# Order of the output products, the 64-row convolution block and the gates in half of the kernel's unit pairs

## The chip, the cores and the metric

The kernel runs on one core of a Trainium2 chip. The metric is device microseconds of one execution, the median of several runs. Lower is better.

## The reference

The input is x, 4 images of 128 channels of 96 x 96. Each image is normalised in 32 groups, then read as four sequences of 9216 positions: by rows, by rows backward, by columns, by columns backward. Every sequence goes through the same block, and the four results are fused by a 1x1 convolution and added to x. The block, cut to what matters:

```python
t = _grouped1x1(x, in_proj_w, in_proj_b, G)
u, gate = (t[:, :HID], t[:, HID:])
u = silu(u)
u = conv1d(u, dw_w, groups=HID)              # 5 taps, per channel
s = _conv1x1(u, ssm_in_w)
a = clip(DMIN + (DMAX - DMIN) * sigmoid(_conv1x1(u, ssm_delta_w, ssm_delta_b)))
bb, cc = tanh(_conv1x1(u, ssm_b_w, ssm_b_b)), tanh(_conv1x1(u, ssm_c_w, ssm_c_b))
hst = exp(prefix) * cumsum(bb * s * exp(-prefix))    # prefix = cumsum(log(a))
u = u + _conv1x1(cc * hst + ssm_d * s, ssm_out_w)
u = _grouped1x1(u * sigmoid(gate), mix_w, mix_b, G)
return _conv1x1(u, out_proj_w, out_proj_b)
```

## The kernel before, in words

**Tiling.** A sequence is cut into 6 stages per phase, and a stage's positions into 4 residues modulo 4 (`R`). One unit is one residue of one stage of one direction: 384 positions by 256 channels, held as two halves `j` of 128 channels. Units come in pairs, one forward and one backward (`s` = 0 and 1). Eight phases (4 images, two reading orders) of 6 stages of 4 pairs make 192 pairs; `pair` runs the first six, `pair_on` the others, one after another. The order of everything is written out by hand under a manual schedule: each engine runs its instructions in the order in which the code issues them.

**What a pair does in `pair_on`.** In the order of the code: the front of a pair four places on (`front`, where it is still to be computed); the five taps of the convolution of half 1 on VectorE and ScalarE (`taps`, L744 and L742); the convolution of half 0 on TensorE, eight products of 128 rows (`conv`, the tile `band`); the recurrence; the copies `under` (L589), which put u of an older pair `bi` into the banks 0 to 3, so that the output of the recurrence is added there; two output products (`add_next`, which calls `accumulate`: eight matmuls with `w_fin` each, and a ScalarE copy `ys` at L862 or L860, which GpSimd or VectorE later adds to `acc`, L879); the rest of the convolution (`conv_less`, the tile `less`, 64 rows) and its copy into u (`copy_u`, L717); the gates' products (`gate`, L557) and the recurrence's output products (`out_of`, L577), each of 32 rows and 128 columns; the gating on VectorE (`gating`, L638); the gates' tanh on ScalarE (L593, L599); and the projection of the new u (`proj`, the tile `main`, 16 products).

**Which pairs.** `fronted` is true where the front is still to be computed, in the first three stages of a phase as seen four pairs ahead. In the other pairs the silu tiles are reused or reloaded, and these compute gates for a pair further on (`gated`). `single` is true for the residues 0 and 3: there half 0 needs just one block of the convolution, and VectorE adds the edge (L691). For the residues 1 and 2 the 64-row block `conv_less` is needed, accumulating into the same banks.

**Banks.** PSUM has 8 banks. In pairs that are not fronted the convolution is in banks 6 and 7, the output products in 4 and 5 (`PROJ`), which the projection uses later; the recurrence's output goes to 0 to 3. The gates go to banks 4 (1, 1), 7 (1, 0), 6 (0, 0) and 5 (0, 1). `copy_u` takes banks 6 and 7 in one copy of 128 x 768.

**Shapes on TensorE.** A matmul takes as many rows of the array as its contraction has, and as many columns as its output has. `accumulate`, `conv` and `proj` are 128 rows by 32 columns, four beside each other; `conv_less` is 64 by 32, eight beside each other; `gate` and `out_of` are 32 by 128, four beside each other, one in each row group. `gate(s, j)` is in row group 2(1 - s) + j, `out_of(s, j)` in row group 2j + s.

Of the kernel before, what the change touches and what calls it, by code (L numbers as in the profile page):

```python
# [68 lines left out]
def conv_preact_kernel(  # L69
# [55 lines left out]
    def bank(i):  # L125
        return psum[:, i, :]

    def mm(o, col, lhsT, rhs, start, stop):
        r = slice(32 * col, 32 * col + 32)
        nc.tensor.matmul(o[r, : rhs.shape[-1]], lhsT, rhs, start=start, stop=stop,  # L130
                         skip_group_check=True)
# [166 lines left out]
    def fresh(step):  # L298

        return step * UB < NU and step % NS < NS // 2  # L300
# [72 lines left out]
    def less_of(p):  # L373
        return 1 if p < 2 else 0

    def less_rows(s, p):
        low = 64 * ((less_of(p) + s + 1) % 2)
        return slice(low, low + 64)
# [174 lines left out]
    def gate(bi, s, j, to):  # L553
        un = units[bi]
        q, off = gate_at(un)
        r = slice(64 * (1 - s) + 32 * j, 64 * (1 - s) + 32 * j + 32)
        nc.tensor.matmul(bank(to)[:, :N], stats[un["b"]][0][r, s, :], x_in[s][r, q, off : off + N],  # L557
                         start=True, stop=True)
# [10 lines left out]
    def ssm(bi, s):  # L569

        k = bi - NU + 8 + s
        return turning[k % 3] if bi >= NU - 8 else SSM + 2 * s

    def out_of(bi, s, j):
        z = tbs[bi]
        r = slice(64 * j + 32 * s, 64 * j + 32 * s + 32)
        nc.tensor.matmul(bank(ssm(bi, s) + j)[:, :N], w_so[r, bass.ts(j, P)], z[r, :],  # L577
                         start=(bi, s) not in seeded, stop=True, skip_group_check=True)
# [7 lines left out]
    def under(bi, s):  # L586

        seeded.add((bi, s))
        nc.scalar.copy(psum[:, ssm(bi, s) : ssm(bi, s) + 2, :N], us[bi][:, s])  # L589
# [52 lines left out]
    def columns(step, sil, k):  # L642

        if fresh(step):
            return sil[..., k : k + N]
        return sil[..., 1 - k : 1 - k + N][..., ::-1]

    def blocks(step):
        return [sils[step][:, s if fresh(step) else 1 - s, 0] for s in range(2)]
# [10 lines left out]
    def alone(p):  # L660
        return p in (0, R - 1)
# [38 lines left out]
    def conv_less(i, banks, copy=True):  # L700
        step, p = units[i]["step"], units[i]["p"]
        sil, k, b0 = blocks(step), less_of(p), min(banks)
        for g in range(4):
            for s in range(2):
                r = less_rows(s, p)
                mm(bank(b0 + s), g, less[r, p, g, :], columns(step, sil[s][r, g, :], k),
                   False, True)
        if copy:
            copy_u(i, banks)

    def copy_u(i, banks):
        b0 = min(banks)
        if banks == PROJ:
            for s in range(2):
                nc.scalar.copy(us[i][:, s, 0, :], bank(b0 + s)[:, :N])
        else:
            nc.scalar.copy(us[i][:, :, 0, :], psum[:, b0 : b0 + 2, :N])  # L717
# [82 lines left out]
    def scale_s(i):  # L800
        s = tbs[i][0:64, :]
        nc.scalar.activation(s, s, AF.Copy, scale=d_sb[0:64, 0:1])
# [92 lines left out]
    def piece(t, place):  # L895
        later.pop((t % NP, place), lambda: None)()
# [58 lines left out]
    def pair_on(t):  # L955
        i, k, n, end = 2 * t, t % R, t - LAG, NU // 2
        bi, last = 2 * n, t == end - 1
        late = n > 1 and (n - 1) % (NP * 2) == 0
        un = units[i]
        single = alone(un["p"])  # L960
        step, g = divmod(t + R, R)
        fronted, gated = fresh(step), None
# [9 lines left out]
        banks, w = (PROJ, FRONT[:2]) if fronted else ((6, 7), PROJ)  # L972
# [31 lines left out]
        def add_next(bk):  # L1004
            if n:
                add = accumulate(waiting.pop(0), bk, *adder)
                held.append(add) if late or k == R - 1 and not last else add()

        add_next(w[0])
        if not fronted:  # L1010
            if not single:
                conv_less(i, banks, False)
            under(bi, 0)
            if not single:
                copy_u(i, banks)
        add_next(w[1])
        if fronted:
            if not single:
                conv_less(i, banks)
            if t % NP == 20:  # L1020
                scale_s(i - 4)
            scale_s(i - 2)

        def gate_of(s, j, bk):
            if gated is not None:
                gate(2 * gated, s, j, bk)
# [2 lines left out]
        out_of(bi, 0, 0)  # L1029
        out_of(bi, 0, 1)  # L1030
        out_of(bi, 1, 1)
        gate_of(1, 0, 7)
        gate_of(0, 0, 6)
        out_of(bi, 1, 0)
        gate_of(0, 1, 5)
        piece(t, 1)
        for s in range(2):
            gating(bi, s)
# [245 lines left out]
    with tc.manual_schedule(  # L1284
        engines={
            nc.tensor.engine, nc.vector.engine, nc.scalar.engine, nc.gpsimd.engine, nc.sync.engine
        }
    ):
        start()
        for t in range(LAG):  # L1290
            pair(t)
        for t in range(LAG, NU // 2):
            pair_on(t)
        tail()
# [82 lines left out]
```

## Time and profile before

| | |
|---|---|
| median of 3 runs | 1737.27 us (1737.03 to 1740.41) |
| span of the profiled execution | 1735.2 us |
| TensorE matmuls busy (PE) | 1713.6 us, 99% |
| weight loads (PEld) | 644.7 us, 37% |
| VectorE (DVE) | 1507.9 us, 87% |
| ScalarE (ACT) | 1494.8 us, 86% |
| GpSimd (POOL) | 1447.0 us, 83% |
| granted TensorE clock | 1.000 |

The profile gives the span, from the first to the last instruction, and no other time of that execution. A row of the timeline has the start in us, the length in us, the engine, the line of the kernel, the operation, the tiles (out<-in), shapes and the count of instructions that are merged in it; in brackets stands how long the engine was idle before it and what ended that. A row that merges matmuls goes from the first start to the last modelled end.

### The profile page before, as it was taken

How to read it: one execution, taken by the hardware profiler on the slowest of the kernel's cores; microseconds unless marked ns; L12 is line 12 of the kernel's file. 1: busy time of each engine (PE TensorE's matmuls, PEld its weight loads, DVE VectorE, ACT ScalarE, POOL GpSimd, SP SyncE). 2: the span in 40 equal slices, each digit the busy share in tenths (PEclk: the TensorE clock that was granted, in tenths of full speed). 3: DMA queues.
4: the chain of work that ended last, by engine and by line, in shares of the span. 5: the costliest groups of instructions: out<-in, count | busy, mean ns of one | idle time of the engine just before them, and what ended most of it. 6: DMA issues, size and time to landing. Idle time of an engine off the chain costs nothing.

```text
span 1735.2 us, 54226 instructions
## 1 busy us (share of the span) xinstructions
PE 1713.6 (99%) x22522; PEld 644.7 (37%) x22522; DVE 1507.9 (87%) x1508; ACT 1494.8 (86%) x2544; POOL 1447.0 (83%) x1490
## 2 busy tenths in 40 slices
PE   7999999999999999999999999999999999999998
PEld 4333333343333433344333443334333333333333
DVE  6899998888889998888889999888888888888887
ACT  4888988889888888888988888888998889888875
POOL 3689889888789988888788988887878889887887
PEclk9999999999999999999999999999999999999999
DMA  7746865358884786337896487433887548643364
GB/s 244 235 147 218 288 202 151 124 206 280 275 287 139 262 267 194 118 126 263 260 308 226 150 300 251 144 123 132 294 294 239 179 144 304 201 137 133 147 226 166
DMA packets 154644, 363.66 MB, mean 210 GB/s; under 512 B 19104, under 2 KB 120864, under 8 KB 154400
## 3 DMA queue, kind: packets, MB, share of 16 engines
q1 hardware_dynamic: 154256, 360.16, 62.8%
q8 instruction: 178, 2.92, 0.7%
q14 instruction: 66, 0.54, 0.1%
q10 hardware_dynamic: 144, 0.04, 0.0%
HBM read 221.41 MB, written 138.53 MB: 207 GB/s over the span
## 4 chain that ended last, share of the span: by engine, by line
PE 95%; DVE 2%; ACT 1%; DMA 1%; issue 0%; SPq 0%; DVEq 0%; ACTq 0%
PE psum L130 81%; PE psum L577 8%; PE psum L557 5%; DVE psum L744 1%; PE psum L1188 0%; DMA acc<-in_xr 0%; DMA kept<-shared 0%; DVE u L638 0%; ACT psum L589 0%; ACT psum L742 0%; DVE u L744 0%; ACT sil L527 0%; SPq L335 0%; PE psum L1195 0%; DVE u L691 0%
## 5 line engine op out<-in xcount | busy, mean ns | idle before, releaser
L744 DVE SCALAR_TENSOR_TENSOR psum<-sil,small,psum 128x768 f32<-128x768 f32 x576 | 589.1, 1023 | 42.2 <-ACT psum L742 16.8
L130 PE MATMUL psum<-u,w_fin 128*32 128x384 f32 (+1 forms) x6192 | 541.3, 484 | 1.1 <-ACT ys L860 0.4
L130 PE MATMUL psum<-u,main 128*32 128x384 f32 x6144 | 535.0, 489 | 0.5 <-DVE u L691 0.4
L638 DVE SCALAR_TENSOR_TENSOR u<-gate,psum 128x768 f32<-128x768 f32 x376 | 341.7, 950 | 150.0 <-PE psum L577 50.8
L879 POOL TENSOR_TENSOR acc<-ys,acc 128x384 f32<-128x384 f32 x375 | 411.8, 1120 | 14.0 <-ACT ys L860 1.9
L825 POOL TENSOR_TENSOR t<-t,t 64x384 f32<-64x384 f32 (+1 forms) x192 | 287.2, 1496 | 70.6 <-DVE t L819 48.3
L589 ACT COPY psum<-u 128x768 f32<-128x768 f32 x384 | 301.4, 799 | 10.5 <-DVE u L638 4.3
L130 PEld LDWEIGHTS psum<-u,w_fin 128*32 128x32 f32 x6192 | 195.2, 109 | 309.6 <-issue 235.5
L130 PEld LDWEIGHTS psum<-u,main 128*32 128x32 f32 x6144 | 180.0, 109 | 324.5 <-issue 218.3
L130 PE MATMUL psum<-sil,band 128*32 128x384 f32 x3072 | 285.3, 488 | 0.0
L792 POOL TENSOR_SCALAR t<-tm 64x384 f32<-64x384 f32 x184 | 170.8, 928 | 114.4 <-ACT tm L781 102.4
L826 POOL TENSOR_TENSOR t<-t,t 64x384 f32<-64x384 f32 (+1 forms) x192 | 233.9, 1218 | 15.1
L793 POOL TENSOR_TENSOR t<-t,tm 64x384 f32<-64x384 f32 x192 | 213.8, 1113 | 30.2 <-ACT t L784 15.5
L577 PE MATMUL psum<-t,main 32*128 32x384 f32 x1536 | 228.1, 525 | 4.2 <-ACT psum L589 4.2
L742 ACT ACTIVATE psum<-sil,small 128x768 f32<-128x768 f32 x191 | 172.6, 904 | 65.2 <-DVE u L638 61.9
L744 DVE SCALAR_TENSOR_TENSOR u<-sil,small,psum 128x768 f32<-128x768 f32 x192 | 194.9, 1015 | 6.8
L527 ACT ACTIVATE sil<-psum,bnorm 128x385 f32<-128x385 f32 x384 | 191.6, 584 | 4.0 <-DMA edge<-sil 0.9
L557 PE MATMUL psum<-x_in,wn 32*128 32x384 f32 x768 | 161.7, 498 | 0.0
L862 ACT COPY ys<-psum 128x384 f32<-128x384 f32 x288 | 132.3, 478 | 33.0 <-PE psum L130 28.3
L130 PEld LDWEIGHTS psum<-sil,band 128*32 128x32 f32 x3072 | 88.8, 108 | 171.4 <-issue 63.1
L781 ACT ACTIVATE tm<-psum,small 128x384 f32<-128x384 f32 x192 | 110.9, 578 | 14.0 <-PE psum L130 2.3
L577 PEld LDWEIGHTS psum<-t,main 32*128 32x128 f32 x1536 | 93.9, 183 | 73.7 <-issue 41.0
(108 smaller groups left out, 1512.3 us busy)
## 6 DMA issues: line engine op xcount, KB each, us to landing
gate<-kept SPq DMA_DIRECT2D x114, 768.0 KB, 5.2
kept<-gate SPq DMA_DIRECT2D x74, 768.0 KB, 3.7
sil<-sil SPq DMA_DIRECT2D x64, 770.0 KB, 6.6
lone<-edge SPq DMA_DIRECT2D x40, 770.0 KB, 7.5
x_in<-in_xs SPq DMA_DIRECT2D x250, 96.2 KB, 3.3
edge<-sil SPq DMA_DIRECT2D x96, 192.5 KB, 3.6
out<-acc SPq DMA_DIRECT2D x46, 384.0 KB, 6.4
acc<-in_xr SPq DMA_DIRECT2D x39, 384.0 KB, 6.4
```

What stands on the lines that cost most here:

```text
L130: nc.tensor.matmul(o[r, : rhs.shape[-1]], lhsT, rhs, start=start, stop=stop, skip_group_check=True)
L527: nc.scalar.activation(sils[step][:, s, j, g, :], bank(bk)[:, : N + 1], AF.Silu, bias=bn[:, 1:2] if j else bn[:, 4 + g : 5 + g],)
L557: nc.tensor.matmul(bank(to)[:, :N], stats[un["b"]][0][r, s, :], x_in[s][r, q, off : off + N], start=True, stop=True)
L577: nc.tensor.matmul(bank(ssm(bi, s) + j)[:, :N], w_so[r, bass.ts(j, P)], z[r, :], start=(bi, s) not in seeded, stop=True, skip_group_check= ...
L589: nc.scalar.copy(psum[:, ssm(bi, s) : ssm(bi, s) + 2, :N], us[bi][:, s])
L638: nc.vector.scalar_tensor_tensor(v, g, 1.0, pz, ALU.add, ALU.mult)
L742: nc.scalar.activation(part, src, AF.Copy, scale=w_tap[:, 0:1])
L744: nc.vector.scalar_tensor_tensor(us[i][:, :, 1, :] if k == K - 1 else part, src, w_tap[:, k : k + 1], part, ALU.mult, ALU.add,)
L793: nc.gpsimd.tensor_mul(ta[0:64, p, :], tb[0:64, :], tm[0:64, :])
L825: engine.tensor_mul(ta[0:64, p, r], tb[64:P, r], ta[64:P, p, r])
L826: engine.tensor_add(tb[0:64, r], ta[0:64, p, r], tb[0:64, r])
L879: adder.tensor_add(part, y, part)
```

## The change

In pairs that are neither fronted nor single, `conv_less` and `copy_u` move behind the second output product, so that both output products stand ahead of the 64-row block and that block directly ahead of the gates. In the same pairs the order of gates and outputs behind it becomes: gate (1, 1); outputs (0, 0), (0, 1), (1, 1), (1, 0); gate (0, 1); and last gates (0, 0) and (1, 0), into the banks 6 and 7 that `copy_u` empties. Single and fronted pairs keep their order.

```diff
         add_next(w[0])
         if not fronted:
-            if not single:
-                conv_less(i, banks, False)
             under(bi, 0)
-            if not single:
-                copy_u(i, banks)
         add_next(w[1])
+        if not fronted and not single:
+            conv_less(i, banks, False)
+            copy_u(i, banks)
...
         out_of(bi, 0, 0)
         out_of(bi, 0, 1)
         out_of(bi, 1, 1)
-        gate_of(1, 0, 7)
-        gate_of(0, 0, 6)
-        out_of(bi, 1, 0)
-        gate_of(0, 1, 5)
+        if single:
+            gate_of(1, 0, 7)
+            gate_of(0, 0, 6)
+            out_of(bi, 1, 0)
+            gate_of(0, 1, 5)
+        else:
+            out_of(bi, 1, 0)
+            gate_of(0, 1, 5)
+            gate_of(0, 0, 6)
+            gate_of(1, 0, 7)
```

On TensorE, one such pair, before; w_fin is the output products, less the 64-row block, x_in the gates (71 for s = 1, 70 for s = 0), t the recurrence's outputs, main the projection, and the brackets name the engines or DMA queues whose semaphore an instruction waits for:

```order
L130 MATMUL psum<-u_1_3_0_904,w_fin 32x384 [waits DVE_49,Activation_49]
L130 MATMUL psum<-u_1_3_0_904,w_fin 32x384 x7
L130 MATMUL psum<-sil_747,less 32x384 x8
L130 MATMUL psum<-u_1_3_0_904,w_fin 32x384 [waits DVE_49,Activation_49]
L130 MATMUL psum<-u_1_3_0_904,w_fin 32x384 x7
L557 MATMUL psum<-x_in_71,wn_269 128x384 [waits DMAHW2_49,Activation_49]
L577 MATMUL psum<-t_0_1_0_0_1036,main 128x384 [waits Activation_49,Pool_49]
L577 MATMUL psum<-t_0_1_0_0_1036,main 128x384 [waits Pool_49]
L577 MATMUL psum<-t_0_1_0_0_1036,main 128x384
L557 MATMUL psum<-x_in_71,wn_269 128x384 [waits Activation_49]
L557 MATMUL psum<-x_in_70,wn_269 128x384 [waits DMAHW1_49]
L577 MATMUL psum<-t_0_1_0_0_1036,main 128x384
```

The last gate, (0, 1), and the projection follow. The same pair in the changed kernel, on TensorE:

```order
L130 MATMUL psum<-u_1_3_0_904,w_fin 32x384 [waits DVE_49,Activation_49]
L130 MATMUL psum<-u_1_3_0_904,w_fin 32x384 x7
L130 MATMUL psum<-u_1_3_0_904,w_fin 32x384 [waits DVE_49,Activation_49]
L130 MATMUL psum<-u_1_3_0_904,w_fin 32x384 x7
L130 MATMUL psum<-sil_747,less 32x384 x8
L557 MATMUL psum<-x_in_71,wn_269 128x384 [waits DMAHW2_49,Activation_49]
L577 MATMUL psum<-t_0_1_0_0_1036,main 128x384 [waits Activation_49,Pool_49]
L577 MATMUL psum<-t_0_1_0_0_1036,main 128x384 [waits Pool_49]
L577 MATMUL psum<-t_0_1_0_0_1036,main 128x384 x2
L557 MATMUL psum<-x_in_70,wn_269 128x384 [waits DMAHW1_49,Activation_49]
L557 MATMUL psum<-x_in_70,wn_269 128x384 [waits Activation_49]
L557 MATMUL psum<-x_in_71,wn_269 128x384
```

The 64-row block has moved behind the second product; the gate that waits for the copy of banks 6 and 7 is now the last but one before the projection, behind all four outputs, and it waits for ScalarE alone.

On ScalarE, at the same place of an earlier pair, L589 is the copy `under`, L862 the copy of an output product, L717 the copy of banks 6 and 7, and L593 a gate's tanh; - is before, + is changed:

```order
 L862 COPY ys_0_2_0_1091<-psum 128x384
 L589 COPY psum<-u_0_3_0_577 128x2x384
+L862 COPY ys_0_2_1_1103<-psum 128x384
 L717 COPY u_2_1_0_1064<-psum 128x2x384
-L862 COPY ys_0_2_1_1112<-psum 128x384
 L593 ACTIVATE gate_177<-psum,bnorm_272 128x384 x2
```

The copy of the second output product now stands ahead of the copy of banks 6 and 7, and that copy directly ahead of the gates' tanh. On VectorE and GpSimd the order of instructions is as before.

## The prediction

> **What bounds the kernel now.** I read the page first, then PE's list of waits, then the timeline of one of the pairs that the change touches, and last the timelines of two kinds of pair that it leaves alone, because they already show the new sequence and the new kind of wait.
>
> ```profile
> span 1735.2 us, 54226 instructions
> PE 1713.6 (99%) x22522; PEld 644.7 (37%) x22522; DVE 1507.9 (87%) x1508; ACT 1494.8 (86%) x2544; POOL 1447.0 (83%) x1490
> ...
> PE 95%; DVE 2%; ACT 1%; DMA 1%; issue 0%; SPq 0%; DVEq 0%; ACTq 0%
> ```
>
> ```profile
> PE psum L577 <- ACT psum L589: 4.2, 6, 1.3
> ```
>
> PE is busy for 99% of the span and carries 95% of the chain that ended last. Apart from one 11.7 us load at the start, its longest total wait is 4.2 us. So a change counts by what it does to PE's own sequence. "Busy" hides two things, though: time lost where the array goes from one tile shape to another, and time in which only some of the four row groups work. Both must be read from start times.
>
> This is a touched pair. PE rows first, then ScalarE (ACT) and VectorE (DVE), all from the timeline:
>
> ```profile
> 301.19 1.47 PE L130 MATMUL psum<-u,w_fin 128*32 128x384 f32 x16
> 302.59 0.88 PE L130 MATMUL psum<-sil,less 64*32 64x384 f32 x16
> 303.39 1.50 PE L130 MATMUL psum<-u,w_fin 128*32 128x384 f32 x16
> 304.82 0.58 PE L557 MATMUL psum<-x_in,wn 32*128 32x384 f32 x1
> 305.25 0.80 PE L577 MATMUL psum<-t,main 32*128 32x384 f32 x4
> 305.58 0.52 PE L557 MATMUL psum<-x_in,wn 32*128 32x384 f32 x3
> 305.90 0.51 PE L557 MATMUL psum<-x_in,wn 32*128 32x384 f32 x3
> 306.40 2.79 PE L130 MATMUL psum<-u,main 128*32 128x384 f32 x32
> ...
> 303.54 0.80 ACT L589 COPY psum<-u 128x768 f32<-128x768 f32 x1
> 304.28 0.79 ACT L717 COPY u<-psum 128x768 f32<-128x768 f32 x1
> 304.97 0.48 ACT L862 COPY ys<-psum 128x384 f32<-128x384 f32 x1
> 305.76 1.31 ACT L593 ACTIVATE gate<-psum,bnorm 128x384 f32<-128x384 f32 x2 [0.31 <-PE psum L577]
> 305.91 1.82 DVE L638 SCALAR_TENSOR_TENSOR u<-gate,psum 128x768 f32<-128x768 f32 x2 [0.56 <-ACT ys L862]
> ```
>
> The trace shows each matmul call as two passes (8 calls, x16), and a block's modelled end lies 0.07 us behind the next block's start (301.19 + 1.47 = 302.66 against 302.59). I count from the first output product, call it 0: the 64-row block starts at 1.40, the second product at 2.20, the gates at 3.63, the projection (u,main) at 5.21. The gate block takes 1.58. Its second half, where a row group gets its second call, starts 0.76 after the first (305.58).
>
> All 47 touched pairs with gates look like this one. The first and the last of them run from first product to projection in 95.04 - 89.81 = 5.23 and 1644.16 - 1638.94 = 5.22; I use 5.22.
>
> ```profile
> 89.81 1.47 PE L130 MATMUL psum<-u,w_fin 128*32 128x384 f32 x16
> 95.04 0.53 PE L130 MATMUL psum<-u,main 128*32 128x384 f32 x4
> ```
>
> ```profile
> 1638.94 1.47 PE L130 MATMUL psum<-u,w_fin 128*32 128x384 f32 x16
> 1644.16 0.53 PE L130 MATMUL psum<-u,main 128*32 128x384 f32 x4
> ```
>
> **The change, part by part.** The instructions are the same in number and kind; nothing is added. `alone` and `fresh` pick the pairs: not fronted and not single are 50 pairs, of which 47 compute gates and 3 at the end of the program don't. This row counts them (51 copies, one of them from the start-up):
>
> ```profile
> L717 ACT COPY u<-psum x51: 792/802/804, 33.1 to 1684.3; 128x768 f32<-128x768 f32 x51
> ```
>
> *What goes: a change of tile shape.* Before, the sequence of shapes is 128x32, 64x32, 128x32, 32x128; now it is 128x32, 64x32, 32x128. The fronted pairs already run it so:
>
> ```profile
> 406.54 2.76 PE L130 MATMUL psum<-u,w_fin 128*32 128x384 f32 x32
> 409.23 0.88 PE L130 MATMUL psum<-sil,less 64*32 64x384 f32 x16
> 410.03 0.93 PE L577 MATMUL psum<-t,main 32*128 32x384 f32 x8
> 410.19 0.86 ACT L715 COPY u<-psum 128x384 f32<-128x384 f32 x2
> ```
>
> There the 64-row block starts 2.69 after the first product and the 32-row block 0.80 after that, at 3.49 instead of 3.63. So the gates would start 0.14 us earlier. If nothing else moved, the projection would start at 3.49 + 1.58 = 5.07, which is 0.15 less than 5.22.
>
> *What comes: a wait for the copy.* The 64-row block ends the convolution in banks 6 and 7. ScalarE copies both out in one instruction (L717), and only then may gates be written there. Before, the second product (1.43 us) stood between the block and the gates, so the copy ended at 305.07, before the first gate into these banks at 305.25 to 305.58. That cover is gone. The new place of the copy is read from the fronted pair: its copy starts at 410.19, 0.09 behind the block's modelled end, that is 3.65 after the first product. ScalarE is free by then: its copy into the accumulating banks (L589) ends at 304.34, 3.15 after the first product, and the second product's copy (L862, 0.48) ends at about 3.6. With 0.80 for L717 the banks are free at 4.45.
>
> Now the release. A gate waiting for a ScalarE copy loaded its weights here, 0.05 after that copy's end (304.97 + 0.48 = 305.45):
>
> ```profile
> 305.50 0.18 PEld L557 LDWEIGHTS psum<-x_in,wn 32*128 32x128 f32 x1
> ```
>
> And this is what follows such a load in an idle row group, in a single pair whose output products waited for a copy that ended at 356.88:
>
> ```profile
> 356.07 0.81 ACT L589 COPY psum<-u 128x768 f32<-128x768 f32 x1
> ```
>
> ```profile
> 356.99 0.47 PEld L577 LDWEIGHTS psum<-t,main 32*128 32x128 f32 x7
> ```
>
> ```profile
> 357.42 0.66 PE L577 MATMUL psum<-t,main 32*128 32x384 f32 x4
> ```
>
> From load to second pass it is 0.43. The second pass takes 0.48 to its modelled end, and the projection starts 0.07 before that, plus 0.01 for the second of the two gates. So the projection starts at 4.45 + 0.05 + 0.43 + 0.48 + 0.01 - 0.07 = **5.35**, against 5.22: **+0.13 us a pair**. Unhindered, the second half would have started at 3.49 + 0.76 = 4.25; its weights now come at 4.50, so the wait of some 0.25 costs more than the crossing gains.
>
> The bounds of this unknown: nothing of the wait felt gives -0.15; and the release at 0.11 behind the copy (356.88 to 356.99, a product that waits for two engines) instead of 0.05 gives +0.19. I take 0.05, since the new first gate behind the copy waits for ScalarE alone, as the one at 305.50 did in that step.
>
> *The rest costs nothing.*
>
> ```profile
> 301.70 0.58 ACT L790 ACTIVATE t<-psum,small 64x384 f32<-64x384 f32 x1
> ```
>
> The second product starts 0.8 us earlier than before, when its bank must be free: the last reader, the tanh L790, ended at 301.70 + 0.58 = 302.28 in this pair, and the product would start at 301.19 + 1.29 = 302.48 (two products take 2.69 with the crossing, one 1.40, so one alone 1.29). The tanh of the first gate (L593, 0.58) now starts behind the copy at 4.45 and ends at about 5.03, ahead of 5.35, so the projection's bank is free. VectorE's gating (L638) needs the first-half products, which come 0.14 earlier. No DMA moves past another on its queue. On ScalarE two copies change places; behind them stand the gates' tanhs, done in time as said.
>
> *The three pairs without gates.* Their projection reads the copied tile at once. Before it is 1652.55 - 1648.05 = 4.50 from the first product; now 4.45 + 0.05 = 4.50. Nothing.
>
> ```profile
> 1648.05 1.47 PE L130 MATMUL psum<-u,w_fin 128*32 128x384 f32 x16
> 1652.55 2.79 PE L130 MATMUL psum<-u,main 128*32 128x384 f32 x32
> ```
>
> **The sum**: 47 x 0.13 = +6.1 us. The span goes from 1735.2 to 1741.3. The profile gives no other time of its own execution; the median of the timed runs, 1737.27, lies 2.1 above the span, and I keep that distance: **1743.4 us**, 0.35% slower. A measurement of this kernel can tell about 0.2% (3.5 us) from no change, so the sign hangs on more than 0.07 us a pair.
>
> **The rivals.**
>
> *Weights in early (no difference).* If the waiting gate's weights were already in the array when the copy ends, the two passes would follow each other as in an unbroken stream, 0.32 apart (305.58 to 305.90) instead of 0.43. That takes 0.11 off: +0.02 a pair, +1 us, 1738.3. Against it: the load itself stood behind the semaphore at 305.50. I give it 0.10. The Trainium skill, "TensorE: Matmul & The Clock Gate", section Architectural detail, says that PE's queue can pull weight loads ahead of matmuls in flight; if that held across a wait for a semaphore, the time would be this rival's 1738.3, while by the row it is the forecast's.
>
> *The copy doesn't hold (faster).* One mechanism: the gates into banks 6 and 7 stand last, six calls behind the block, and if ScalarE were done before their turn, only the crossing would be left. It decides at 4.25 - 0.05 = 4.20 for the copy's end. Then 50 x 0.15 = 7.5 us go: 1729.8. For it: gates last is as late as they can stand. Against it: the six calls fill only one and a half rounds of four row groups, and start plus length of the copy, both rows of this trace, give 4.45. Chance 0.07.
>
> *ScalarE held up by GpSimd (much slower).* The second product's copy L862 now stands ahead of L717, and in every second touched pair it also waits for a buffer that GpSimd's add (L879) frees. Where that came too late, L717 would wait behind it.
>
> ```profile
> 589.82 2.40 POOL L879 TENSOR_TENSOR acc<-ys,acc 128x384 f32<-128x384 f32 x2
> ```
>
> ```profile
> 594.79 0.48 ACT L862 COPY ys<-psum 128x384 f32<-128x384 f32 x1 [0.24 <-PE psum L130]
> ```
>
> The add ended at 592.22, the copy would come about 1 us before 594.79; 1.6 us are left. If it stayed where it was, L717 would start 0.6 later in 24 pairs: +14 us on top, 1758. Chance 0.04.
>
> **How the numbers follow.** Forecast 0.74; the three rivals 0.10, 0.07, 0.04; 0.05 for what I don't see. The range goes from the rival without a difference (1738.0) to what a release slower than either row here would give, +0.23 a pair (1748.0); it leaves out the faster case, the GpSimd case and some of the unseen. Faster: 0.07 and 0.01 of the unseen. Same: 0.10 and 0.03 from the low end of the forecast. Slower: the rest, 0.79.
>
> **What the profile after would show.** The 64-row block 2.69 behind the first product and the gates 0.80 behind it prove the gain. L717 starting at 3.65, the second half of the gates with a weight load at 4.50 and the projection at 5.35 prove the loss; a projection at 5.07 refutes it, and one at 5.24 means that weights came early. Distances in fronted and single pairs must stay (2.69 and 0.80 in the rows above). A projection later than 5.5 would mean that ScalarE came late: then L862 or L589 ends after 3.65.

## The result, and the profile after

| | before | changed |
|---|---|---|
| median of 5 runs each | 1737.27 us (1736.7 to 1740.41) | 1743.62 us (1743.29 to 1743.81) |
| ratio | | 1.0034, 95% interval 1.0022 to 1.0046 |
| span of the profiled execution | 1735.2 us | 1741.6 us |

The change made the kernel 0.34% slower. The page of the changed kernel, its head and its chain:

```profile
span 1741.6 us, 54289 instructions
PE 1720.4 (99%) x22522; PEld 660.8 (38%) x22522; DVE 1509.4 (87%) x1508; ACT 1499.2 (86%) x2544; POOL 1448.2 (83%) x1490
...
PE 95%; DVE 2%; ACT 1%; issue 0%; DMA 0%; POOL 0%; SPq 0%; DVEq 0%; POOLq 0%
```

The page doesn't show where the time went. TensorE runs the same 22522 matmuls, and its busy time rises with the span (by 6.8 us), because a stretch in which two of four row groups work and two wait counts as busy. Its list of waits has no entry for the copy either. What tells is the timeline of the pair that the prediction shows, the same pair in the changed kernel: TensorE, then ScalarE and VectorE.

```profile
302.39 2.76 PE L130 MATMUL psum<-u,w_fin 128*32 128x384 f32 x32
305.08 0.88 PE L130 MATMUL psum<-sil,less 64*32 64x384 f32 x16
305.89 0.58 PE L557 MATMUL psum<-x_in,wn 32*128 32x384 f32 x1
306.32 0.80 PE L577 MATMUL psum<-t,main 32*128 32x384 f32 x4
306.66 0.85 PE L557 MATMUL psum<-x_in,wn 32*128 32x384 f32 x3
306.98 0.85 PE L557 MATMUL psum<-x_in,wn 32*128 32x384 f32 x3
307.76 0.53 PE L130 MATMUL psum<-u,main 128*32 128x384 f32 x4
...
304.75 0.80 ACT L589 COPY psum<-u 128x768 f32<-128x768 f32 x1
305.49 0.47 ACT L862 COPY ys<-psum 128x384 f32<-128x384 f32 x1
306.07 0.80 ACT L717 COPY u<-psum 128x768 f32<-128x768 f32 x1
306.84 1.27 ACT L593 ACTIVATE gate<-psum,bnorm 128x384 f32<-128x384 f32 x2
306.99 1.82 DVE L638 SCALAR_TENSOR_TENSOR u<-gate,psum 128x768 f32<-128x768 f32 x2 [0.42 <-ACT u L717]
```

And the weight loads of the two gates that wait for the copy:

```profile
306.92 0.19 PEld L557 LDWEIGHTS psum<-x_in,wn 32*128 32x128 f32 x2
```

Counted again from the first output product: the 64-row block starts at 2.69, the 32-row block at 3.50 instead of 3.63. The copy runs from 3.68 to 4.48, the two gates load their weights at 4.53, and the projection starts at 5.37 instead of 5.22. The two rows of gates are 0.85 long where they were 0.52 and 0.51: each merges a pass that starts on time with passes of the late gates. All 47 touched pairs with gates have the projection at 5.37 or 5.38.

### The profile page after: what moved, and what is told of

It is laid out like the page before. It is cut to its first block, busy times and chain, and to the rows that moved or that the text cites. A ratio compares the mean times of both kernels' runs of the same rounds, so it can differ in the third digit from the quotient of the medians.

```text
span 1741.6 us, 54289 instructions
## 1 busy us (share of the span) xinstructions
PE 1720.4 (99%) x22522; PEld 660.8 (38%) x22522; DVE 1509.4 (87%) x1508; ACT 1499.2 (86%) x2544; POOL 1448.2 (83%) x1490
## 4 chain that ended last, share of the span: by engine, by line
PE 95%; DVE 2%; ACT 1%; issue 0%; DMA 0%; POOL 0%; SPq 0%; DVEq 0%; POOLq 0%
PE psum L130 80%; PE psum L577 7%; PE psum L557 7%; DVE psum L744 1%; DMA acc<-in_xr 0%; PE psum L1193 0%; DVE u L638 0%; ACT psum L589 0%; DVE u L744 0%; ACT psum L742 0%; ACT sil L527 0%; SPq L335 0%; POOL t L825 0%; PE psum L1200 0%; DVE u L691 0%
## 5 line engine op out<-in xcount | busy, mean ns | idle before, releaser
L130 PE MATMUL psum<-u,w_fin 128*32 128x384 f32 (+1 forms) x6192 | 531.0, 483 | 1.1 <-ACT ys L860 0.4
L130 PEld LDWEIGHTS psum<-u,w_fin 128*32 128x32 f32 x6192 | 200.4, 109 | 297.5 <-issue 254.0
L589 ACT COPY psum<-u 128x768 f32<-128x768 f32 x384 | 301.3, 799 | 9.9 <-DVE u L638 4.3
L557 PE MATMUL psum<-x_in,wn 32*128 32x384 f32 x768 | 177.1, 508 | 0.0
L862 ACT COPY ys<-psum 128x384 f32<-128x384 f32 x288 | 132.6, 479 | 25.2 <-PE psum L130 16.3
```

## The experiments

Where a time in a pair is given below, it is counted from the pair's first output product, and "the projection" is its start. In the kernel before it is at 5.22, in the changed one at 5.37.

| kernel | projection, us | median, us | ratio to before (95% interval) |
|---|---|---|---|
| gate_order_only | 5.22 | 1737.71 | 0.9997 (0.9987 to 1.0008) |
| block_moved_only | 5.38, 5.39 | 1744.92 | 1.0051 (1.0032 to 1.0071) |
| copy_split_on_scalar | 5.41 | 1746.04 | 1.0049 (1.0034 to 1.0064) |
| copy_twice | 6.20, 6.21 | 1784.74 | 1.0274 (1.0255 to 1.0292) |
| half_copied_ahead | 5.08 (40 of 47 pairs) | 1731.92 | 0.9970 (0.9957 to 0.9982) |
| copy_ahead_of_block | 5.08 (40 of 47 pairs) | 1734.54 | 0.9982 (0.9973 to 0.9991) |
| two_engines_every_second | 5.22 to 5.97 | 1741.42 | 1.0026 (1.0017 to 1.0036) |

The theory under test is that of the prediction: the crossing saved is worth some 0.15 us a pair, and the end of the copy of banks 6 and 7 decides what is left of it. The rivals are those of the prediction, and that the order of the gates matters by itself.

**block_moved_only**, against the changed kernel:

```diff
-        if single:
-            gate_of(1, 0, 7)
-            gate_of(0, 0, 6)
-            out_of(bi, 1, 0)
-            gate_of(0, 1, 5)
-        else:
-            out_of(bi, 1, 0)
-            gate_of(0, 1, 5)
-            gate_of(0, 0, 6)
-            gate_of(1, 0, 7)
+        gate_of(1, 0, 7)
+        gate_of(0, 0, 6)
+        out_of(bi, 1, 0)
+        gate_of(0, 1, 5)
```

> The 64-row block and its copy stand behind the second output product as in the change, but the gates keep their old order, so that gate (1, 0), which needs bank 7, is the fifth call and the output (1, 0) and gate (0, 1) stand behind it. Theory (the end of the copy of banks 6 and 7 sets when the second half of the 32-row block starts): that half starts as one, 0.05 us behind the copy, and the projection comes 5.37 us after the first output product, as in the changed kernel; time as changed, 1743.6, within 1 us. Rival (the new order of the gates hides part of the wait): without it the four calls behind the copy take longer than the two of the changed kernel, the projection comes 0.1 or more later and the time is 1748 or more.

Measured: the projection at 5.38 or 5.39, the span 1743.0, 1.4 above the changed kernel's. The timeline of a pair whose first product is at 312.04, ScalarE's copy and then the weight loads:

```profile
315.71 0.80 ACT L717 COPY u<-psum 128x768 f32<-128x768 f32 x1 [0.31 <-PE psum L130]
```

```profile
316.56 0.19 PEld L557 LDWEIGHTS psum<-x_in,wn 32*128 32x128 f32 x2 [0.71 <-ACT u L717]
316.57 0.18 PEld L577 LDWEIGHTS psum<-t,main 32*128 32x128 f32 x1
316.58 0.18 PEld L557 LDWEIGHTS psum<-x_in,wn 32*128 32x128 f32 x1
```

The copy ends at 316.51 and all four second-half calls load their weights 0.05 to 0.07 behind it, the output and gate (0, 1) too, which stand behind the blocked gate in the queue and had no reason of their own to wait: in the changed kernel, where they stand ahead of it, they load their weights at 3.93 and 3.95. The projection comes only 0.014 later than in the changed kernel. So the block's move makes the loss, and by the traces the new order of the gates gives back about 0.65 us of it (47 x 0.014); the rest of the 1.4 lies outside the touched pairs. The timed runs can't tell the two kernels apart: the median is 1.3 us higher, a little more than the 1 us expected, and the intervals of the two ratios overlap.

**gate_order_only**, against the kernel before, the other half of the change:

```diff
-        gate_of(1, 0, 7)
-        gate_of(0, 0, 6)
-        out_of(bi, 1, 0)
-        gate_of(0, 1, 5)
+        if single:
+            ...
+        else:
+            out_of(bi, 1, 0)
+            gate_of(0, 1, 5)
+            gate_of(0, 0, 6)
+            gate_of(1, 0, 7)
```

> The block stays between the two output products as before; only the order of the gates is the new one. Theory: the copy has ended before the gates start, so no gate waits for it; the projection stays at 5.22 us after the first product and the time at that of before, 1737.3, within 1 us. Rival (the new order itself costs, since gate (0, 1), which waits for the second product's copy, now stands ahead of two others): their weights come at about 305.5 instead of 305.26 in the pair shown, the second half starts up to 0.05 later, 2 us in 47 pairs, 1739.6.

Measured: the ratio's interval holds 1, and the projection is between 5.21 and 5.25 in all 47 pairs, at 5.22 in 41 of them. The order costs nothing where the copy has ended.

**copy_ahead_of_block**, against the changed kernel:

```diff
+        if not fronted and not single:
+            copy_u(i, banks)
         add_next(w[0])
...
             conv_less(i, banks, False)
-            copy_u(i, banks)
```

> As the changed kernel, but the copy of banks 6 and 7 is issued ahead of the first output product, so it copies the convolution without the 64-row block: that part of the convolution is left out of u in 50 pairs. All instructions are still there; only the wait of the gates for the copy goes. Theory: the block starts 2.69 and the gates 3.49 to 3.50 us after the first product, nothing holds them, and the projection comes at 5.07 to 5.10; 47 pairs by 0.27 to 0.30 less than changed, so 1729.5 to 1731. Rival (the loss is not the wait but the new sequence of shapes or the order of gates): the projection stays near 5.37 and the time near 1743.6.

Measured: TensorE, one of the 40 pairs with the projection at 5.08, and ScalarE's tanh of its gates:

```profile
336.62 2.76 PE L130 MATMUL psum<-u,w_fin 128*32 128x384 f32 x32
339.32 0.88 PE L130 MATMUL psum<-sil,less 64*32 64x384 f32 x16
340.12 0.58 PE L557 MATMUL psum<-x_in,wn 32*128 32x384 f32 x1
340.88 0.49 PE L557 MATMUL psum<-x_in,wn 32*128 32x384 f32 x3
341.20 0.49 PE L557 MATMUL psum<-x_in,wn 32*128 32x384 f32 x3
341.70 0.53 PE L130 MATMUL psum<-u,main 128*32 128x384 f32 x4
```

```profile
341.07 1.27 ACT L593 ACTIVATE gate<-psum,bnorm 128x384 f32<-128x384 f32 x2 [0.75 <-PE psum L577]
```

Without the wait the second half starts 0.76 behind the first, and the pair is 0.14 shorter than before: the crossing is worth what the forecast says. The time is 3.1 us below that of before (1737.60 in the runs beside it), not 6 to 8. Part of the rest went where the copy was put: in seven pairs, the first touched one of every phase but the first, ScalarE's queue is late already, the early copy pushes the end of the copy `under` to 3.84 and the projection to 5.47 or later. I had not counted that. So the 47 pairs together are 3.7 us shorter than before up to the projection, not 6.6 (47 x 0.14). Another 1.0 us is lost behind the projection, in nine pairs, as the last section shows.

**half_copied_ahead**, against the changed kernel, keeps the mechanism and takes only half of the copy away from behind the block:

```diff
+        if not fronted and not single:
+            nc.scalar.copy(us[i][:, :, 0, N // 2 :], psum[:, 6:8, N // 2 : N])
         add_next(w[0])
...
             conv_less(i, banks, False)
-            copy_u(i, banks)
+            nc.scalar.copy(us[i][:, :, 0, : N // 2], psum[:, 6:8, : N // 2])
```

> As the changed kernel, but half of the columns of banks 6 and 7 are copied ahead of the first output product, so in those columns u lacks the 64-row part of the convolution; only the other half (128 x 2 x 192) is copied behind the block. Theory: such a copy takes about 0.48 us, as long as the copies of 128 x 384 in this trace, starts at 3.67 and ends at 4.15, ahead of the 4.20 at which it would hold nothing; the projection comes at 5.08 in most of the pairs and the time is 1730.5 to 1734, as with the whole copy ahead of the block (1734.5, where the first pair of each image lost 0.26 to the longer queue on ScalarE). Rival (any gate that waits for ScalarE behind the block costs a fixed amount): the projection stays above 5.2 and the time above 1737.

Measured: ScalarE and then TensorE, a pair whose first product is at 336.38:

```profile
340.05 0.48 ACT L1017 COPY u<-psum 128x384 f32<-128x384 f32 x1 [0.31 <-PE psum L130]
340.82 1.27 ACT L593 ACTIVATE gate<-psum,bnorm 128x384 f32<-128x384 f32 x2 [0.28 <-PE psum L577]
```

```profile
340.63 0.55 PE L557 MATMUL psum<-x_in,wn 32*128 32x384 f32 x3
341.45 0.53 PE L130 MATMUL psum<-u,main 128*32 128x384 f32 x4
```

The copy still stands behind the block and the gates still wait for ScalarE, but it ends at 340.53, that is 4.15, and the projection is at 5.07. A wait that ends in time costs nothing; no fixed price hangs on it.

The seven pairs that the table leaves out are again the first touched one of every phase but the first. ScalarE comes late there, here in a pair whose first product is at 301.79:

```profile
305.58 0.50 ACT L1017 COPY u<-psum 128x384 f32<-128x384 f32 x1
306.99 0.53 PE L130 MATMUL psum<-u,main 128*32 128x384 f32 x4
```

The copy ends at 306.08 = 4.29, and the projection stands 0.9 behind it, at 5.20, as it does in the changed kernel (4.48 and 5.37). The outputs are late in these pairs too (from 3.66 on instead of 3.50), so what an end of 4.29 costs by itself is not shown.

**copy_twice**, against the changed kernel:

```diff
             copy_u(i, banks)
+            copy_u(i, banks)
```

> As the changed kernel, with the copy of banks 6 and 7 made twice in the 50 pairs. Theory: the projection follows the end of the copy one to one. In the trace ScalarE starts an instruction 0.07 us ahead of the recorded end of the one before, so the second copy ends 0.73 later, the projection comes at 6.10 instead of 5.37, and 50 x 0.73 = 36 us are added: 1780. Rival (other work hides part of a longer wait): a slope well under 1, under 1770.

Measured: ScalarE and TensorE, a pair whose first product is at 317.43:

```profile
321.11 1.63 ACT L717 COPY u<-psum 128x768 f32<-128x768 f32 x2 [0.31 <-PE psum L130]
```

```profile
322.79 0.92 PE L557 MATMUL psum<-x_in,wn 32*128 32x384 f32 x4 [0.29 <-ACT u L717]
323.63 0.53 PE L130 MATMUL psum<-u,main 128*32 128x384 f32 x4
```

The copies end at 322.74, 5.31 behind the first product, 0.83 later than one copy, since the second starts 0.03 behind the end of the first and not 0.07 ahead of it. It writes the very place that the first writes; whether that is the reason was not tested by itself, but two copies into different halves of u overlap by 0.10 (copy_split_on_scalar). The projection is at 6.20, 0.83 later than 5.37: the slope is 1. My 1780 took 0.73 for the second copy; 50 x 0.83 = 41.5 on 1743.6 is 1785.1, and 1784.74 was measured. This wait is long enough to be seen as idle time of TensorE (0.29).

**copy_split_on_scalar**, against the changed kernel:

```diff
-            copy_u(i, banks)
+            for s in range(2):
+                nc.scalar.copy(us[i][:, s, 0, :], bank(6 + s)[:, :N])
```

> As the changed kernel, but ScalarE copies bank 6 and bank 7 in two instructions. In the fronted pairs two such copies run from the first start to the last end in 0.86 us, against 0.80 for one copy of both. Theory (the last of the two gates sets the projection): gate (0, 0) loads its weights 0.3 earlier, gate (1, 0) 0.06 later, the projection comes 0.06 later at 5.43, 47 x 0.06 = 2.8 us on top of the changed kernel, 1746.4. Rival (the first release decides, since the second gate's row group could run on its own): up to 0.25 earlier, 1732 to 1740.

Measured: the span 1743.9 and the projection at 5.41 in all 47 pairs. ScalarE, a pair whose first product is at 312.00, and its projection:

```profile
315.66 0.86 ACT L1016 COPY u<-psum 128x384 f32<-128x384 f32 x2 [0.29 <-PE psum L130]
```

```profile
317.42 0.53 PE L130 MATMUL psum<-u,main 128*32 128x384 f32 x4
```

And the weight load of gate (0, 0):

```profile
316.19 0.18 PEld L557 LDWEIGHTS psum<-x_in,wn 32*128 32x128 f32 x1
```

The second copy ends at 316.52 = 4.52, 0.04 later than the single one, and the projection comes 0.04 later. Gate (0, 0), whose bank was free 0.3 earlier, loads its weights at 4.19 instead of 4.53 and gains nothing for the pair. The last release decides.

**two_engines_every_second**, against the kernel before; `k` is the residue's place in its stage, 0 or 1 in the pairs that are not single:

```diff
         if not fronted:
-            if not single:
+            if k == 0:
                 conv_less(i, banks, False)
             under(bi, 0)
-            if not single:
+            if k == 0:
                 copy_u(i, banks)
         add_next(w[1])
+        if not fronted and not single and k == 1:
+            conv_less(i, banks, False)
+            nc.scalar.copy(us[i][:, 0, 0, :], bank(6)[:, :N])
+            nc.vector.tensor_copy(us[i][:, 1, 0, :], bank(7)[:, :N])
...
+        if single or k == 0:
...
+        else:
...
```

The cut leaves out the gates: in the old order where `single or k == 0`, in that of the changed kernel otherwise.

> An attempt at a better kernel with the whole computation: the new order only where VectorE ends its scan early (the second residue of a stage, 24 of the 50 pairs), with bank 6 copied by ScalarE and bank 7 by VectorE beside each other; the old order in the other 26. In the changed kernel VectorE's scan ends there 3.5 to 3.9 us after the first product. ScalarE's half ends at 4.15; VectorE's takes 0.55 (its copies of this size in the start-up) and ends at 4.22 to 4.5. Theory: the projection comes 0.9 behind the later end, at 5.12 to 5.4, where it was 5.22: about nothing in sum, 1736.5 to 1739. Rival (two engines reading PSUM beside each other slow each other down, or VectorE's later gating holds the taps): more than 1740.

Measured: 1741.42, slower than before and outside my range. ScalarE and VectorE in a pair whose first product is at 523.39, one of those where VectorE's scan ends earliest:

```profile
525.24 1.81 DVE L819 TENSOR_TENSOR_SCAN t<-t 64x768 f32<-64x768 f32 x1
527.05 0.48 ACT L1019 COPY u<-psum 128x384 f32<-128x384 f32 x1 [0.30 <-PE psum L130]
527.16 0.56 DVE L1020 COPY u<-psum 128x384 f32<-128x384 f32 x1
```

VectorE's copy ends at 527.72 = 4.33, and the projection is at 5.22, just that of before. The new order stands in 25 pairs, not 24, and 23 of them compute gates. In six of the 23 the projection is at 5.22; in 16 the scan ends later than I had read from the changed kernel, the copy with it, and the projection is at 5.3 to 5.6, and in one at 5.97. In all 23 it follows the later copy's end by 0.89, so the mechanism held and my reading of when VectorE is free did not; why the scan ends later is not shown. The time is in the rival's range, but not by its mechanisms: the copies beside each other took 0.48 and 0.56, as forecast, and the 23 pairs' longer way to the projection, 4.3 us in sum, is all that the span rose by (1735.2 to 1739.5). No kernel here that computes all of u is faster than the one before.

## Why the prediction was right, point by point

- **What goes** was right: the block at 2.69, the gates at 3.50 (forecast 3.49). The gain if nothing holds, 0.15, came out as 0.14 in the two kernels in which the copy holds nothing.
- **What comes** was right in its kind and place, and each number within 0.03: copy's start 3.68 (3.65), its end 4.48 (4.45), the weight loads 4.53 (4.50), the projection 5.37 (5.35). The term that was a little small is the copy's start: 0.11 behind the block's modelled end, where the fronted pair had 0.09. ScalarE's idle time before it makes no difference, since the 47 copies start at 3.67 or 3.68 whether ScalarE had been idle for 0.03 us or for 0.37. What differs is the copy itself: the fronted pair's first copy reads one bank, as do those of copy_split_on_scalar, which start at 3.66, and L717 reads both. Why that costs 0.02 is not shown. A pair loses 0.15, not 0.13.
- **The release** at 0.05, which I chose against 0.11, was the right one of the two rows.
- **The rest costs nothing** held: fronted and single pairs keep their distances (2.69 and 0.80; 1.67 for a single pair's gate block), and VectorE's gating starts 4.60 behind the first product in the pair shown, instead of 4.72. The bracket of its row names the copy L717 as the last to end, but the gating doesn't hang on it: with the copy made twice it still starts at 4.59 to 4.61 in most pairs.
- **The pairs without gates**: 4.53 instead of the 4.50 forecast, by the same 0.03.
- **The sum** is closer to the time than its terms deserve. The way to the projection grew by 7.2 us in the 47 pairs together, where the forecast had 6.1, and the span rose by 6.4, since 0.8 us went away elsewhere. Most of that, 0.7, is one pair outside the touched ones, which in the profiled execution of before holds a wait of 0.59 us that the one of after doesn't have; why it went is not shown. That the small term and this nearly cancel is luck. The wait in TensorE's timeline of before:

```profile
616.09 1.05 PE L130 MATMUL psum<-x_in,wn 32*32 32x385 f32 x32 [0.59 <-ACT shared L599]
```

- **Weights in early** fell: the loads stand 0.05 behind the copy's end in the changed kernel and in block_moved_only, and the second pass follows at 0.43.
- **The copy doesn't hold** fell for the changed kernel, and its price and its point of decision, 4.20, proved right elsewhere: with the copy's end at 4.15 (half_copied_ahead) the pair is at 5.08, with 4.48 at 5.37, with 5.31 at 6.20.
- **ScalarE held up by GpSimd** fell: L862 ended by 3.64 in all 47 touched pairs, and L717 never started later than 3.68.

## What to carry to other kernels

A crossing between tile shapes can be saved by moving a block, but ask what the block's neighbour was covering: here 1.4 us of products hid a copy of 0.8 us, and without them 0.29 us of it came to light (5.37 against 5.08) for a crossing of 0.14. Price such a move from pairs of the same kernel that already run the new sequence, end of copy plus a measured tail, rather than from busy time, which doesn't show a row group that waits. When the banks were released in parts, only the last part counted (copy_split_on_scalar).

## What the runs showed that I had not expected

- The next bounds lie close behind. Without the wait the projection stops at 5.08, not at 5.00: in copy_ahead_of_block the second passes end at 341.69, and by the distance of 0.07 the projection could start at 341.62; the first gate's tanh (341.07 + 0.58 = 341.65) holds its bank until 0.05 before 341.70. The kernel before has this bound too, and the prediction carried it along in its 1.58 without naming it: in the pair shown there the tanh ends at 305.76 + 0.58 = 306.34, and the projection's weights come 0.06 behind it.

```profile
306.40 0.16 PEld L130 LDWEIGHTS psum<-u,main 128*32 128x32 f32 x8 [0.60 <-ACT gate L593]
```

- In half_copied_ahead, in the nine pairs where VectorE's scan ends last (at 4.97 to 5.00), 0.1 us of the gain is lost again before the next pair. ScalarE and TensorE there, the scan having taken 3.09:

```profile
548.74 3.09 DVE L819 TENSOR_TENSOR_SCAN t<-t,t 64x768 f32<-64x768 f32 x1
551.86 1.82 DVE L638 SCALAR_TENSOR_TENSOR u<-gate,psum 128x768 f32<-128x768 f32 x2
552.85 0.91 ACT L742 ACTIVATE psum<-sil,small 128x768 f32<-128x768 f32 x1 [0.29 <-DVE u L638]
553.69 0.88 ACT L599 ACTIVATE gate<-psum,bnorm 128x768 f32<-128x768 f32 x1
554.62 0.16 PEld L130 LDWEIGHTS psum<-sil,band 128*32 128x32 f32 x8 [0.61 <-ACT gate L599]
```

  The gating waits for the scan, the tap for the gating, the tanh of banks 6 and 7 for its turn behind the tap, and the next convolution loads its weights 0.05 behind that tanh (553.69 + 0.88 = 554.57), 2.70 behind the projection instead of 2.60.
- A call blocked in TensorE's queue holds those behind it even where their own operands and banks are free (block_moved_only, weights at 4.53 instead of 3.93), while the calls ahead of it go on: in the pair of the result section gate (0, 1) starts a pass at 306.66, when the two late gates behind it still wait for 306.92.
